# Work at the seam between two convs of a layer and in the closing sums: other engines, other order, other places

## The chip, the cores and the metric

The kernel runs on one core of a Trainium2 chip. The metric is the device time of one execution in microseconds. PE is TensorE, DVE is VectorE, ACT is ScalarE, POOL is GpSimd and SP is SyncE, which here issues nearly all DMAs.

## The reference

Two layers work on x of shape (4, 64, 256, 256). Each is `x = x + layer(gn(x))` with a group norm over pairs of channels. The change touches only layer 1:

```python
def _L1_conv_ref(x, ...):            # x is the normed input
    identity = x
    h = _conv3x3(x, _quantize_weight(w1), b1)
    h = relu(_batchnorm(h, gamma1, beta1))     # mean and variance over batch and space
    h = _conv3x3(h, _quantize_weight(w2), b2)
    h = _batchnorm(h, gamma2, beta2)
    return relu(h + identity)
x = x + _L1_conv_ref(_gn(x), ...)
```

Because a batch norm takes its mean over the whole batch, no value of the second conv can start before the first conv has ended, and no output before the second has.

## The kernel before

Rows of an image are handled in pairs; an image has 16 chunks of 8 row pairs, and a chunk is a tile of 128 partitions (two halves of 64 channels) by 8 x 256 numbers, 1 MiB. Chunks of the four images make 64 chunks. y is the result of layer 0, kept in HBM (`y_d`).

**First conv of layer 1.** It is laid out in `plan`, a table of steps and orders within a step (`at(step, order, call, ...)`), which five engines are then kept to. For each chunk: `conv1_differences` (GpSimd, L342), `conv1_upper_odd` and `conv1_upper` (ACT), `conv1_lower_odd` (DVE, L361) and `conv1_lower` (DVE, L352) build the tiles for PE; `conv1_odd` and `conv1_even` are the matmuls (L295), `conv1_shared` and `conv1_out` (L317, DVE) bring results to SBUF and add up the sums. `conv1_square` (ACT, Square at L381 with an accumulator) adds up the squares and issues the store of the chunk to `h1_d` from ACT's queue. After the last chunk of an image, `conv1_end` is one more row (six matmuls), `conv1_end_out` its result and its Square, and `conv1_close` reduces sums and squares (L388, L389). In before, the Square of the last chunk is placed behind the end row's.

**The seam.** `bn_affine(bn1, ...)` makes the scale and shift `ss1` of the first batch norm in a chain of small instructions on DVE, PE and ACT. Then the second conv starts. The first chunk has no earlier chunk to hide behind: its rows are scaled by `conv2_affine(0, "odd")` and `conv2_affine(0, "rest")` on ACT (L1264), GpSimd clears a pad row (L1267), `conv2_differences` makes two differences, one on DVE and one on GpSimd (L342), `conv2_upper_odd` copies the odd rows on ACT (L358), `conv2_lower_odd` (DVE, L361) makes the rounded remainder of the odd rows, `conv2_upper` and `conv2_lower` the same for the differences (L345, L350). PE's first three matmuls need the upper odd rows, the next nine the lower ones.

**Second conv.** A loop over 64 chunks in an order written out by hand for all five engines. The tiles for PE are six half tiles of 8256 bytes per partition (`diffs2`, `odds2`, for even and odd chunks) in a pool `halves2`, with `junk2` (the unread output of the Squares), `raw` and `m` tiles behind them. Results go to 14 places (`KEEP`); the first 50 chunks are also stored to `h2_d`, the last 14 stay in SBUF.

**The end.** After the second batch norm's scale `ss2` is known, every chunk becomes `y + relu(ss2 * h + shift + gn * y)`. The pool `end` takes the room of `halves2`, whose tiles it may overwrite one by one as they come free. y is loaded to three places of the ring of input tiles and to `MORE` places in `end`. The order over chunks starts with the 14 kept ones; for the others h is loaded from `h2_d`. SP issues in program order: a load that waits for its place holds up all behind it.

Of the kernel before, what the change touches and what calls it, by code (L numbers as in the profile page):

```python
# [41 lines left out]
def conv_preact_kernel(ctx: ExitStack, tc: tile.TileContext, io, col128, colset, col64):  # L42
# [25 lines left out]
    def flat(t):  # L68
        return t.rearrange("p a b -> p (a b)")
# [26 lines left out]
    def odd_tiles(pool, name, bufs, rows=CPAIR + 1):  # L96

        t = half_pads([half_tile(pool, f"odd_{name}", bufs, rows=rows)])[0]
        return [t[:, 4 * u : 4 * u + 4] for u in range(2)]

    def difference_tiles(pool, name, bufs, rows=CPAIR + 1):
        return half_pads([half_tile(pool, f"diff_{name}{u}", bufs, rows=rows) for u in range(2)])
# [17 lines left out]
    def at(step, order, call, *args):  # L120
        plan[step, order].append((call, args))
# [830 lines left out]
        if g:  # L952
            del m_in[b, k]

    def conv1_square(b, k):
        h = h_out.pop((b, k))
        square("h1", h[:, 1:, :] if k == 0 else h, junks[0], squares[b][:, k : k + 1])
        if k == 0:
            square("h1", h[0:C, 0:1, :], junks[0], squares[b][0:C, NCH : NCH + 1], slice(0, C))
        nc.scalar.dma_start(h1_d[b][:, k * CPAIR : (k + 1) * CPAIR, :], h)  # L960
# [220 lines left out]
    def plan_conv1(b):  # L1181
        t = CONV1 + b * (NG + 1)
        if b == 0:
            at(t - 4, -1, conv1_first)
            at(t, 12, conv1_open)
        for k in range(NCH):
            T = t + 4 * k
            places = [T + p for p in (-13, -7, -6, -5, -4, -4, -4, -3)]
            if b == 0 and k < 3:
                places = [t + p for p in ((-6, -3, -3, -2, -2, -2, -1, -1), (-4, -1, -1, 0, 0, 0, 0, 1), (-2, 1, 2, 3, 4, 4, 4, 5))[k]]  # L1190
            load, diff, odd, up0, up1, low_odd, low0, low1 = places

            first = b == k == 0

            def late(step, order):
                return (step, 5.5 + (order - 13) if step < t else order)

            at(load, 0, conv1_load, b, k)
            at(*late(diff, 13.08), conv1_differences, b, k)
            at(*late(odd, 13.36 if b == 0 and k == 3 else 13.1), conv1_upper_odd, b, k)  # L1200
            at(*late(up0, 13.12), conv1_upper, b, k, 0)
            at(*late(up1, 13.14), conv1_upper, b, k, 1)
            at(*late(low_odd, 13.2), conv1_lower_odd, b, k)
            at(*((t, 1.3) if first else late(low0, 13.22)), conv1_lower, b, k, 0)
            at(*((t, 1.32) if first else late(low1, 13.24)), conv1_lower, b, k, 1)
            at(T, 1.9 if first else 13, conv1_odd, b, k)
            at(T + 4 / 3, 13, conv1_even, b, k, 0)
            at(T + 4 / 3, 13.15, conv1_shared, b, k)
            at(T + 8 / 3, 13, conv1_even, b, k, 1)
            at(T + 8 / 3, 13.05, conv1_out, b, k, 0)  # L1210
            at(T + 4, 13.05 if k < NCH - 1 else 12.9, conv1_out, b, k, 1)
            at(T + 4 + 4 / 3, 13.16, conv1_square, b, k)
        at(t + NG, 12.95, conv1_end, b)
        at(t + NG + 1, 13.06, conv1_end_out, b)
        at(t + NG + 3, 13.3, conv1_close, b)
# [39 lines left out]
    def conv2_load(i):  # L1255
        b, k = chunks[i]
        h = h_in[i] = dense_in(f"h_{b}_{k}", CPAIR + 1)
        nc.sync.dma_start(h, h1_d[b][:, k * CPAIR : (k + 1) * CPAIR + 1, :])

    def conv2_affine(i, part=None):  # L1260
        b, k = chunks[i]
        (even, odd), _ = second_rows(h_in[i])
        for rows in {None: (h_in[i],), "odd": (odd,), "rest": (even, h_in[i][:, CPAIR, :])}[part]:
            nc.scalar.activation(rows, rows, AF.Relu, bias=ss1[:, 1:2], scale=ss1[:, 0:1])  # L1264
        if part != "odd":
            if k == 0:
                nc.gpsimd.memset(h_in[i][C:P, 0, :], 0.0)  # L1267
            if k == NCH - 1:
                nc.gpsimd.memset(h_in[i][0:C, CPAIR, :], 0.0)

    def conv2_differences(i, engines=(nc.gpsimd, nc.gpsimd)):
        for n, engine in enumerate(engines):
            raw_in[i, n] = halves_pool.tile([P, 4, W], F32, tag="raw", name=f"d2_{i}_{n}", bufs=2)
            differences(second_rows(h_in[i])[n], raw_in[i, n], engine)
# [7 lines left out]
    def conv2_upper_odd(i):  # L1282
        upper_odd(odds2[i % 2], second_rows(h_in[i])[1][0])
# [10 lines left out]
    kept = ctx.enter_context(tc.tile_pool(name="kept", bufs=1, reuse_waits="tile"))  # L1294
    halves_stack = ExitStack()
    halves_pool = halves_stack.enter_context(tc.tile_pool(name="halves2", bufs=1, reuse_waits="tile"))
    diffs2 = [difference_tiles(halves_pool, f"2{i}", 6, CPAIR) for i in range(2)]
    odds2 = [odd_tiles(halves_pool, f"2{i}", 6, CPAIR) for i in range(2)]
    junk2 = halves_pool.tile([P, CPAIR * W], BF16, name="junk_2")
    h2, h2_place = {}, count()  # L1300

    def chunk_h2(b, k):
        n = next(h2_place) % KEEP
# [6 lines left out]
    def conv2_odd(i):  # L1310
        b, k = chunks[i]
        if k == 0:
            totals_open(b)
        open_m[i] = bank("ap"[i % 2], f"ps_h2m_{i}")
        convolve_odd(open_m[i], "w2", odds2[i % 2])
# [29 lines left out]
    with tc.manual_schedule(  # L1345
        engines={
            mybir.EngineType.PE,
            mybir.EngineType.SP,
            mybir.EngineType.DVE,
            mybir.EngineType.Pool,  # L1350
            mybir.EngineType.Activation,
        }
    ):
        n = len(chunks)
        conv2_affine(0, "odd")
        conv2_upper_odd(0)
        conv2_affine(0, "rest")
        conv2_differences(0, (nc.vector, nc.gpsimd))
        conv2_lower_odd(0)
        conv2_upper(0, 0)  # L1360
        conv2_upper(0, 1)
        conv2_affine(1)
        conv2_lower(0, 0)
        conv2_lower(0, 1)
        conv2_differences(1)
        conv2_upper_odd(1)
        for i in range(n):
            conv2_odd(i)
            if i:
                conv2_out(i - 1, 1)  # L1370
            if i + 3 < n:
                conv2_load(i + 3)
            if i + 1 < n:
                conv2_upper(i + 1, 0)
                conv2_upper(i + 1, 1)
                conv2_lower_odd(i + 1)
                conv2_lower(i + 1, 0)
                conv2_lower(i + 1, 1)
            if i + 2 < n:
                conv2_affine(i + 2)  # L1380
                conv2_differences(i + 2)
            conv2_shared(i)
            if i:
                conv2_square(i - 1)
            conv2_even(i, 0)
            conv2_out(i, 0)
            if i + 2 < n:
                conv2_upper_odd(i + 2)
            conv2_even(i, 1)
        conv2_square(n - 1, 0, 4, 1)  # L1390
        conv2_out(n - 1, 1)
        conv2_square(n - 1, 4, CPAIR)

    steps = chunks[-KEEP:] + chunks[:-KEEP]
    shift = const.tile([P, B], F32, name="shift")
    ss2 = const.tile([P, 2], F32, name="ss2")
    y_of = {}

    halves_stack.close()
    end = ctx.enter_context(tc.tile_pool(name="end", bufs=2, reuse_waits="tile"))  # L1400
    MORE = 6
    AHEAD = 3 + MORE - 1

    def end_load(i):
        b, k = steps[i]
        if i % (3 + MORE) < 3:
            y_of[i] = dense_in(f"y_end_{b}_{k}", CPAIR)
        else:
            y_of[i] = end.tile([P, CPAIR, W], F32, tag="y", name=f"y_end_{b}_{k}", bufs=MORE)
        nc.sync.dma_start(y_of[i], y_d[b][:, k * CPAIR : (k + 1) * CPAIR, :])  # L1410

    for i in range(AHEAD):
        end_load(i)
    bn_affine(bn2, "g2", "be2", ss2, "bn2")
    for b in range(B):
        nc.vector.tensor_scalar(shift[:, b : b + 1], gn2[b][:, 2:3], ss2[:, 1:2], None, ALU.add)
    for i, (b, k) in enumerate(steps):
        if i + AHEAD < len(steps):
            end_load(i + AHEAD)
        y, h = y_of.pop(i), h2.pop((b, k))  # L1420
        v = end.tile([P, CPAIR, W], F32, tag="v", name=f"v_{b}_{k}")
        nc.scalar.activation(v, y, AF.Identity, bias=shift[:, b : b + 1], scale=gn2[b][:, 1:2])  # L1422
        nc.vector.scalar_tensor_tensor(h, h, ss2[:, 0:1], v, ALU.mult, ALU.add)  # L1423
        nc.vector.scalar_tensor_tensor(h, h, 0.0, y, ALU.max, ALU.add)
        nc.sync.dma_start(io["out"][b, k], flat(h))

        j = i - 3 + KEEP
        if i >= 3 and j < len(steps):
            b2, k2 = steps[j]
            nc.sync.dma_start(chunk_h2(b2, k2), h2_d[b2][:, k2 * CPAIR : (k2 + 1) * CPAIR, :])  # L1430

def _packed(parts, rows):

# [107 lines left out]
```

## Time and profile before

| | |
|---|---|
| time before, median of 3 runs | 3026.77 us (3007.64 to 3039.1) |
| profiled execution | 3016.92 us |
| its span | 3015.1 us |
| PE busy | 2357.4 us (78%) |
| DVE busy | 2478.0 us (82%) |
| ACT busy | 2054.8 us (68%) |
| POOL busy | 1676.3 us (56%) |
| DMA, mean over the span | 304 GB/s, 915.35 MB |

In the profile, times are microseconds from the start of the span. A line of the timeline gives start, duration, engine, source line, operation, output and inputs with shapes, the number of merged instructions and, in brackets, the idle time before it and what ended it. A line of a stretch gives its bounds and length, busy time and instruction count of PE, of weight loads, of DVE, ACT and POOL, then PE's granted clock, the mean busy share of the 16 DMA engines and GB/s. A line of the waits gives who waited for whom, the total, the number of times and the longest.

### The profile page before, as it was taken

To read this page: it belongs to the slowest core of one execution; us is meant where nothing else is said; L and a number is where in the kernel's file an instruction comes from. 1 tells how busy PE (TensorE), PEld (TensorE's weight loads), DVE (VectorE), ACT (ScalarE), POOL (GpSimd) and SP (SyncE) were. 2 spreads that over 40 slices of the span, in tenths; PEclk is the share of its full clock that TensorE was granted. 3 is DMA by queue.
4 is the path that set the end of the run, shared out by engine and by line. 5 is a ranking of instruction groups with operands and counts; after the bars stand their busy time and mean duration, and the time that the engine had idled before them with its cause. 6 is when DMAs were issued, how large, how long until landed. Compare 5 with 4: busy or idle time off the path is not lost.

```text
span 3015.1 us, 52987 instructions
## 1 busy us (share of the span) xinstructions
PE 2357.4 (78%) x21576; PEld 1503.4 (50%) x21576; DVE 2478.0 (82%) x2793; ACT 2054.8 (68%) x2274; POOL 1676.3 (56%) x1210
## 2 busy tenths in 40 slices
PE   1898899998999999988999999989999999000000
PEld 1444444444544445546666667867888888000000
DVE  5678688888888999968988989979999898876665
ACT  6898887787876555557667667868888887422222
POOL 5888887776877778744445546635555555000000
PEclk9999999999999999998999999989999999555555
DMA  8565479999999879848999897746777764899999
GB/s 345 191 249 224 184 259 376 350 342 352 336 343 324 303 288 326 293 147 310 366 356 352 321 345 300 267 178 255 263 266 264 265 232 144 351 411 409 421 427 409
DMA packets 135572, 915.35 MB, mean 304 GB/s; under 512 B 14944, under 2 KB 15712, under 8 KB 40608
## 3 DMA queue, kind: packets, MB, share of 16 engines
q1 hardware_dynamic: 126112, 844.85, 75.0%
q10 hardware_dynamic: 9216, 67.11, 5.5%
q8 instruction: 169, 2.77, 0.4%
q14 instruction: 75, 0.61, 0.1%
HBM read 573.74 MB, written 338.17 MB: 302 GB/s over the span
## 4 chain that ended last, share of the span: by engine, by line
PE 28%; DMA 18%; DVE 5%; issue 2%; ACT 1%; POOL 0%; SPq 0%; DVEq 0%; ACTq 0%; POOLq 0%
PE ps_h L295 18%; PE ps_h2m L295 6%; DMA y_end<-y_d 5%; DMA h<-h_d 4%; DMA out<-h 4%; PE ps_hm L295 3%; DMA y<-in_xp 2%; DVE diff L352 1%; PE ps_o L492 1%; DMA y_d<-y 1%; DVE h L317 1%; DMA h_d<-h 1%; DMA yn<-y_d 1%; DMA xs_in<-xs_d 1%; DVE odd L361 1%
## 5 line engine op out<-in xcount | busy, mean ns | idle before, releaser
L295 PE MATMUL ps_h<-diff,w_q 128*128 128x512 f32 x3072 | 753.8, 400 | 14.3 <-DVE h L317 13.7
L295 PEld LDWEIGHTS ps_h<-diff,w_q 128*128 128x128 f32 x3072 | 576.6, 189 | 192.1 <-issue 23.7
L492 PE MATMUL ps_c<-v,us 64*64 64x256 f32 x9216 | 544.6, 385 | 42.2 <-DVE ps_c L623 36.4
L342 POOL TENSOR_TENSOR d<-yn 128x1024 f32<-128x1024 f32 x128 | 356.0, 2801 | 305.3 <-DMA yn<-y_d 188.5
L492 PEld LDWEIGHTS ps_c<-v,us 64*64 64x64 f32 x9216 | 361.3, 136 | 200.4 <-DVE ps_c L623 45.6
L342 POOL TENSOR_TENSOR d<-h 128x1024 f32<-128x1024 f32 x127 | 311.9, 2477 | 194.8 <-DVE diff L350 133.4
L492 PE MATMUL ps_a<-h,av 64*64 64x512 f32 x4080 | 386.8, 492 | 34.8 <-DVE t L686 23.9
L317 DVE SCALAR_TENSOR_TENSOR h<-ps_h,scale_w,m 128x1024 f32<-128x1024 f32 x256 | 322.8, 1279 | 76.6 <-PE ps_h L295 53.9
L540 POOL TENSOR_TENSOR x<-x 128x512 f32<-128x512 f32 x256 | 329.9, 1289 | 12.3
L1422 ACT ACTIVATE v<-y_end,shift,gn 128x2048 f32<-128x2048 f32 x64 | 133.8, 2092 | 285.1 <-DMA y_end<-y_d 249.9
L492 PEld LDWEIGHTS ps_a<-h,av 64*64 64x64 f32 x4080 | 154.2, 133 | 302.6 <-issue 195.6
L381 ACT ACTIVATE junk<-h,less_h 128x2048 bf16<-128x2048 f32 (+3 forms) x133 | 256.0, 1925 | 11.1 <-DVE h L317 11.0
L1423 DVE SCALAR_TENSOR_TENSOR h<-h,ss,v 128x2048 f32<-128x2048 f32 x64 | 149.8, 2349 | 126.1 <-ACT v L1422 102.1
L683 DVE SCALAR_TENSOR_TENSOR t<-ps_a,m,t 128x1020 f32<-128x1020 f32 x128 | 163.3, 1276 | 103.1 <-ACT t L677 101.1
L848 DVE SCALAR_TENSOR_TENSOR y<-ps_o,ob,y 128x1024 f32<-128x1024 f32 x128 | 163.7, 1279 | 80.6 <-DMA y<-in_xp 27.4
L677 ACT ACTIVATE t<-ps_a,tap_bias,m 128x1024 f32<-128x1024 f32 x128 | 154.0, 1203 | 97.5 <-PE ps_a L492 96.9
L705 ACT ACTIVATE xs<-t 128x1024 f32<-128x1024 f32 x128 | 134.9, 1054 | 116.8 <-DVE t L689 86.8
L352 DVE SCALAR_TENSOR_TENSOR diff<-d,gn,diff 128x1024 fp32r<-128x1024 f32 x128 | 208.5, 1658 | 0.3 <-ACT diff L345 0.3
L295 PE MATMUL ps_hm<-odd,w_q 128*128 128x512 f32 x768 | 194.0, 402 | 8.6 <-ACT m L311 6.0
L295 PE MATMUL ps_h2m<-odd,w_q 128*128 128x512 f32 x768 | 193.2, 400 | 8.2 <-DVE odd L361 4.4
L345 ACT ACTIVATE diff<-d 128x1024 fp32r<-128x1024 f32 x128 | 135.1, 1055 | 83.4 <-POOL d L342 82.2
L532 POOL TENSOR_TENSOR x<-x,x 128x512 f32<-128x512 f32 x128 | 160.7, 1278 | 43.3 <-ACT x L526 43.3
(226 smaller groups left out, 4306.5 us busy)
## 6 DMA issues: line engine op xcount, KB each, us to landing
x<-in_xc SPq DMA_DIRECT2D x64, 1280.0 KB
h<-h_d SPq DMA_DIRECT2D x64, 1152.0 KB
yn<-y_d SPq DMA_DIRECT2D x60, 1152.0 KB
xs_in<-in_xp SPq DMA_DIRECT2D x64, 1024.0 KB
xs_d<-xs SPq DMA_DIRECT2D x128, 512.0 KB
xs_in<-xs_d SPq DMA_DIRECT2D x64, 1024.0 KB
y<-in_xp SPq DMA_DIRECT2D x64, 1024.0 KB
y_d<-y SPq DMA_DIRECT2D x64, 1024.0 KB
```

Source lines behind the costliest of these rows:

```text
L295: nc.tensor.matmul(ps, wq[w][:, kind, kx, :], t[:, rows, kx : kx + W], start=(j == 0), stop=(j == len(terms) - 1))
L317: nc.vector.scalar_tensor_tensor(h.rearrange("p (e k) w -> p e (k w)", e=2), ps.rearrange("p e k w -> p e (k w)"), w_scale[w], m.unsqueeze ...
L342: engine.tensor_tensor(raw.rearrange("p (g r) w -> p g r w", g=2), *pair, ALU.subtract)
L352: nc.vector.scalar_tensor_tensor(lower, raw, scale, upper.bitcast(F32), ALU.mult, ALU.subtract)
L381: nc.scalar.activation(junk[rows, 0:n], flat(h), AF.Square, bias=less[name][rows], accum_out=total)
L492: last[:] = [nc.tensor.matmul(ps[o, at_out[0] : at_out[1], :], w[i], rhs[i], **flags)]
L532: nc.gpsimd.tensor_tensor(x4[:, j - 1], x_rows(u, j + 2), x4[:, j - 1], ALU.subtract)
L540: nc.gpsimd.tensor_tensor(x[:, r : r + 2], x[:, r + 2 : r + 4], x[:, r : r + 2], ALU.subtract)
L677: nc.scalar.activation(flat(t), flat(ps), AF.Identity, bias=tap_bias, scale=sh[:, 1:2])
L683: nc.vector.scalar_tensor_tensor(t[:, :, 1:W], ps[:, :, 0 : W - 1], sh[:, 0:1], t[:, :, 1:W], ALU.mult, ALU.add)
L848: nc.vector.scalar_tensor_tensor(y, ps.rearrange("p x s w -> p x (s w)"), out_bias[b], y, ALU.add, ALU.add)
L1423: nc.vector.scalar_tensor_tensor(h, h, ss2[:, 0:1], v, ALU.mult, ALU.add)
```

## The change

At the first conv's end, the last chunk's Square is made in two halves, each placed right behind the result it reads and ahead of the end row; the second half issues the store. At the start of the second conv, the first chunk's even rows and last row are scaled and cut off at zero on DVE (`conv2_affine_vector`), which also clears the pad row and makes both differences; ACT keeps the odd rows. The half tiles are allocated in another order, odd tiles ahead of the difference tiles of the same parity.

At the end, the two-input sum with a scaled y (`v`) is replaced: with `inverse = ss2 / gn` the first sum is `h * inverse + y` in place of h, ACT then makes `relu(gn * that + shift)` in place, and the second sum adds y. The tile `v` is gone and y has 8 places in `end` in place of 6. Reciprocal and copy for the new scales are done at chunk 8 of the second conv. The first chunk of the end is done in halves, and the order of SP, DVE and ACT is now written out: the first sum of chunk i+1 goes ahead of the second sum of chunk i.

```diff
-    def conv1_square(b, k):
+    def conv1_square(b, k, part=None):
+        if part is not None:
+            h = h_out[b, k][:, 4 * part : 4 * part + 4, :]
+            square("h1", h, junks[0], squares[b][:, k + 2 * part : k + 2 * part + 1])
+            if part:
+                nc.scalar.dma_start(h1_d[b][:, k * CPAIR : (k + 1) * CPAIR, :], h_out.pop((b, k)))
+            return
...
-            at(T + 4 + 4 / 3, 13.16, conv1_square, b, k)
+            if (b, k) == (B - 1, NCH - 1):
+                at(T + 4, 12.85, conv1_square, b, k, 0)
+                at(T + 4, 12.92, conv1_square, b, k, 1)
+            else:
+                at(T + 4 + 4 / 3, 13.16, conv1_square, b, k)
...
+    def conv2_affine_vector(i):
+
+        (even, _), _ = second_rows(h_in[i])
+        for rows in (even, h_in[i][:, CPAIR, :]):
+            nc.vector.tensor_scalar(rows, rows, ss1[:, 0:1], ss1[:, 1:2], ALU.mult, ALU.add)
+            nc.vector.tensor_scalar(rows, rows, 0.0, None, ALU.max)
+        nc.vector.memset(h_in[i][C:P, 0, :], 0.0)
...
-    diffs2 = [difference_tiles(halves_pool, f"2{i}", 6, CPAIR) for i in range(2)]
-    odds2 = [odd_tiles(halves_pool, f"2{i}", 6, CPAIR) for i in range(2)]
+    diffs2, odds2 = [], []
+    for i in range(2):
+        odds2.append(odd_tiles(halves_pool, f"2{i}", 6, CPAIR))
+        diffs2.append(difference_tiles(halves_pool, f"2{i}", 6, CPAIR))
...
+    def end_scales():
+        for b in range(B):
+            nc.vector.reciprocal(inverse[:, b : b + 1], gn2[b][:, 1:2])
+            nc.vector.tensor_copy(shift[:, b : b + 1], gn2[b][:, 2:3])
...
         conv2_affine(0, "odd")
+        conv2_affine_vector(0)
+        conv2_differences(0, (nc.vector, nc.vector))
         conv2_upper_odd(0)
-        conv2_affine(0, "rest")
-        conv2_differences(0, (nc.vector, nc.gpsimd))
         conv2_lower_odd(0)
...
         for i in range(n):
+            if i == 8:
+                end_scales()
...
-    MORE = 6
+    MORE = 8
     AHEAD = 3 + MORE - 1
...
+    def end_sum(i):
+
+        b = steps[i][0]
+        h, y = h2[steps[i]], y_of[i]
+        for a, e in end_parts(i):
+            at_h = h[:, a:e, :]
+            nc.vector.scalar_tensor_tensor(at_h, at_h, inverse[:, b : b + 1], y[:, a:e, :], ALU.mult, ALU.add)
+            nc.scalar.activation(at_h, at_h, AF.Relu, bias=shift[:, b : b + 1], scale=gn2[b][:, 1:2])
+
+    def end_out(i):
+        b, k = steps[i]
+        h, y = h2.pop((b, k)), y_of.pop(i)
+        for a, e in end_parts(i):
+            at_h = h[:, a:e, :]
+            nc.vector.tensor_tensor(at_h, at_h, y[:, a:e, :], ALU.add)
+            nc.sync.dma_start(io["out"][b, k, :, a * W : e * W], flat(at_h))
...
-    for b in range(B):
-        nc.vector.tensor_scalar(shift[:, b : b + 1], gn2[b][:, 2:3], ss2[:, 1:2], None, ALU.add)
-    for i, (b, k) in enumerate(steps):
-        if i + AHEAD < len(steps):
+    nc.vector.tensor_scalar(inverse, inverse, ss2[:, 0:1], None, ALU.mult)
+    nc.vector.tensor_scalar(shift, shift, ss2[:, 1:2], None, ALU.add)
+    with tc.manual_schedule(
+        engines={mybir.EngineType.SP, mybir.EngineType.DVE, mybir.EngineType.Activation}
+    ):
+        end_sum(0)
+        for i in range(len(steps)):
+            if i + 1 < len(steps):
+                end_sum(i + 1)
             end_load(i + AHEAD)
-        y, h = y_of.pop(i), h2.pop((b, k))
-        v = end.tile([P, CPAIR, W], F32, tag="v", name=f"v_{b}_{k}")
-        nc.scalar.activation(v, y, AF.Identity, bias=shift[:, b : b + 1], scale=gn2[b][:, 1:2])
-        nc.vector.scalar_tensor_tensor(h, h, ss2[:, 0:1], v, ALU.mult, ALU.add)
-        nc.vector.scalar_tensor_tensor(h, h, 0.0, y, ALU.max, ALU.add)
-        nc.sync.dma_start(io["out"][b, k], flat(h))
-
-        j = i - 3 + KEEP
-        if i >= 3 and j < len(steps):
-            b2, k2 = steps[j]
-            nc.sync.dma_start(chunk_h2(b2, k2), h2_d[b2][:, k2 * CPAIR : (k2 + 1) * CPAIR, :])
+            end_out(i)
+            j = i - 3 + KEEP
+            if i >= 3 and j < len(steps):
+                b, k = steps[j]
+                nc.sync.dma_start(chunk_h2(b, k), h2_d[b][:, k * CPAIR : (k + 1) * CPAIR, :])
```

More of the change, by code (lines that the diff above doesn't have):

```diff
@@ L1296, in conv_preact_kernel @@
     halves_pool = halves_stack.enter_context(tc.tile_pool(name="halves2", bufs=1, reuse_waits="tile"))
-    diffs2 = [difference_tiles(halves_pool, f"2{i}", 6, CPAIR) for i in range(2)]
-    odds2 = [odd_tiles(halves_pool, f"2{i}", 6, CPAIR) for i in range(2)]
+    diffs2, odds2 = [], []
+    for i in range(2):
+        odds2.append(odd_tiles(halves_pool, f"2{i}", 6, CPAIR))
+        diffs2.append(difference_tiles(halves_pool, f"2{i}", 6, CPAIR))
     junk2 = halves_pool.tile([P, CPAIR * W], BF16, name="junk_2")
     h2, h2_place = {}, count()
+    inverse = const.tile([P, B], F32, name="inverse")
+    shift = const.tile([P, B], F32, name="shift")
+    def end_scales():
+        for b in range(B):
+            nc.vector.reciprocal(inverse[:, b : b + 1], gn2[b][:, 1:2])
+            nc.vector.tensor_copy(shift[:, b : b + 1], gn2[b][:, 2:3])
     def chunk_h2(b, k):
@@ L1394, in conv_preact_kernel @@
     steps = chunks[-KEEP:] + chunks[:-KEEP]
-    shift = const.tile([P, B], F32, name="shift")
     ss2 = const.tile([P, 2], F32, name="ss2")
@@ L1400, in conv_preact_kernel @@
     end = ctx.enter_context(tc.tile_pool(name="end", bufs=2, reuse_waits="tile"))
-    MORE = 6
+    MORE = 8
     AHEAD = 3 + MORE - 1
     def end_load(i):
+        if i >= len(steps):
+            return
         b, k = steps[i]
@@ L1410, in end_load, with end_parts @@
         nc.sync.dma_start(y_of[i], y_d[b][:, k * CPAIR : (k + 1) * CPAIR, :])
+    def end_parts(i):
+        return ((0, CPAIR // 2), (CPAIR // 2, CPAIR)) if i == 0 else ((0, CPAIR),)
+    def end_sum(i):
[12 more added lines that the diff above has]
+            nc.sync.dma_start(io["out"][b, k, :, a * W : e * W], flat(at_h))
     for i in range(AHEAD):
```

## The prediction

> **What bounds the kernel now.** I read the page's slices first, then the chain of waits, then the two places the change touches by their timelines, waits and stretches.
>
> ```profile
> PE   1898899998999999988999999989999999000000
> DMA  8565479999999879848999897746777764899999
> GB/s 345 191 249 224 184 259 376 350 342 352 336 343 324 303 288 326 293 147 310 366 356 352 321 345 300 267 178 255 263 266 264 265 232 144 351 411 409 421 427 409
> ```
>
> A slice is 75.4 us. Until slice 34 PE is full; in the last six PE does nothing and DMA moves 351 to 427 GB/s. So there are two regimes: in the second conv a microsecond counts if PE waits for it; in the end only if the DMA engines stand still. The chain of waits agrees: matmuls to 2563.5, then only DMAs to the end.
>
> Between the convs PE has no conv work from 2008.7. This is the timeline there (start, duration, engine, what ended the idle time before):
>
> ```profile
> 2008.02 1.28 DVE L317 SCALAR_TENSOR_TENSOR h<-ps_h,scale_w,m 128x1024 f32<-128x1024 f32 x1 [1.47 <-PE ps_h L295]
> 2010.49 2.00 ACT L381 ACTIVATE junk<-h,less_h 128x2048 bf16<-128x2048 f32 x1
> 2012.61 0.19 DVE L389 TENSOR_REDUCE sum_h<-squares 128x1 f32<-128x34 f32 x1 [2.17 <-ACT junk L381]
> 2016.87 1.24 ACT L1264 ACTIVATE h<-h,ss 128x1024 f32<-128x1024 f32 x1 [0.81 <-DVE ss L1250]
> 2020.84 1.23 DVE L342 TENSOR_TENSOR d<-h 128x1024 f32<-128x1024 f32 x1 [4.00 <-POOL h L1267]
> 2021.01 3.25 POOL L342 TENSOR_TENSOR d<-h 128x1024 f32<-128x1024 f32 x1 [0.21 <-ACT h L1264]
> 2021.98 3.37 DVE L361 TENSOR_TENSOR odd<-h,odd 128x1024 fp32r<-128x1024 f32 x1
> 2025.40 4.21 PE L295 MATMUL ps_h2m<-odd,w_q 128*128 128x512 f32 x9 [4.44 <-DVE odd L361]
> ```
>
> Two steps stand out: VectorE waits 2.17 us for the last Square before the sums can close, and the first odd difference (L361) takes 3.37 us beside GpSimd's difference. PE resumes at 2025.40, 8.5 us after the scale `ss` is there (2016.84).
>
> At the end the DMA share (the column before GB/s) falls once all loads are in:
>
> ```profile
> 2563.00:2566.00 3.00, 3.00 (x15) 2.39 (x14) 1.35 (x1) 1.22 (x2) 0.00 (x0) 1.00 0.34 145
> 2566.00:2569.00 3.00, 3.00 (x14) 2.18 (x12) 1.29 (x2) 1.24 (x2) 0.00 (x0) 1.00 0.00 0
> 2580.00:2582.00 2.00, 0.00 (x0) 0.00 (x0) 2.00 (x2) 1.56 (x2) 0.00 (x0) 0.50 1.01 426
> 2582.00:2584.00 2.00, 0.00 (x0) 0.00 (x0) 2.00 (x2) 1.83 (x2) 0.00 (x0) 0.50 0.22 90
> 2584.00:2586.00 2.00, 0.00 (x0) 0.00 (x0) 2.00 (x2) 1.76 (x1) 0.00 (x0) 0.50 0.00 0
> ```
>
> The first hole is loads that wait for a place, the second the wait for the first store. SP's own waits name the first:
>
> ```profile
> SPq L1410 <- DVE odd L361: 24.2, 3, 8.1
> SPq L1410 <- PE ps_h L295: 13.2, 3, 8.0
> ```
>
> Afterwards a step has three 1 MiB transfers and takes 7.37 us (stores issued at 2942.80 and 2950.16), 2.46 us each; in it VectorE works 4.64 us and ACT 2.09. Neither sets the pace.
>
> **The Trainium skill.** "DMA: Bandwidth & Descriptors", Where 436 GB/s comes from, gives a ceiling of 435 GB/s for the 16 engines; the trace's 427 from 2830 to 3010 is within 2% of it, so fewer instructions cannot shorten that stretch. "SBUF — State Buffer", Who interferes with whom: a VectorE operation with two SBUF inputs and a GpSimd one that reads SBUF exclude each other. The trace agrees: L361 takes 3.37 us here, 1.22 at least elsewhere. "TensorE: Matmul & The Clock Gate", What's actually happening: half clock after about 3.4 us of idling; here the nine matmuls take 0.47 us each, against 5.80/24 = 0.24 later. Price: "VectorE: DVE Perf Modes", The perf-mode tier table, has fp32 `tensor_scalar` from SBUF at twice the rate of `tensor_tensor`, 1227 ns for 2048 elements; the trace has only shorter ones or such as ran beside GpSimd.
>
> **The change, part by part.**
>
> *Squares in halves.* The first half's Square runs while PE does the last group. The second follows the last L317: 2009.30 + 0.09 + 1.15 (a half Square in the second conv's last chunk: 1.15) = 2010.54, then the end row's Square (0.50) and its accumulator read (0.18): the reduce starts near 2011.3 instead of 2012.61. ACT's issue of the store of h, between the two, can hold that up by 0.33. Gain 1.0 to 1.3; I take **1.2**. ACT was idle 4.22 us there, so the first half costs nothing.
>
> *First chunk on VectorE.* From `ss` on, before: ACT affine, odd tile, affine rest, GpSimd memset, differences, L361 ends after 8.5 us. Now on VectorE: multiply-add and max of 1024 elements, the same of 256, a memset, two differences, L361. By the skill's rate a 1024 `tensor_scalar` is (512+150)/0.96 = 0.69 us, a 256 one 0.29 (estimates from that page): 2 x 0.69 + 2 x 0.29 + 0.3 = 2.3. Then 2 x 1.23 + 1.22 = 3.7, together 6.0, say 6.2 with the waits between. At full-length rate (L313: 1.33 per 1024, from PSUM; 0.42 per 256, L910) the front part is 3.8 and the sum 7.5. ACT's own steps (1.24 and 1.06) are done by then. Gain 8.5 - 6.2 = **2.3**, low end 1.0. Moved behind it: the second Copy and the affine of chunk 1 on ACT, then GpSimd's differences of chunk 1. The affine began at 2025.26, 8.4 us after `ss`; now at about 6.0. So it advances with PE and no new wait comes up. Matmuls stay at half clock. From then on PE waited 0.8 us in the whole second conv, so the gain reaches its end.
>
> *Eight small VectorE instructions at chunk 8.* 8 x 0.2 = 1.6 us. VectorE is 99% busy there, but PE's next bank is ready early: even group at 2098.45, its bank read by 2096.53. 1.9 us of cover; I take 0, at worst 1.6.
>
> *Places at the end.* In the compiled program of before, a tag's first place is its lowest and the next go from its highest down. That puts the second y place over one of chunk 63's difference tiles, which is why the fifth load waited 8.0 us, to 2568.46. By the same rule the new order gives: first place over chunk 62's odd tile (free at 2555.1), second over raw tiles and chunk 62's m (2562), third over `junk_2`, which the last Square writes until 2571.7. SP issues in order, so loads 6 to 11 all wait for that Square. They then move without a gap, from 2572.5 for 6 x 2.46 = 14.8 us, to 2587.3. Before, nine loads were in at 2582.4, and by 2587.3 0.4 of a store: 9.4 transfers against 11. Gain 1.6 x 2.46 = **3.9 us**. The transfers number 64 + 50 + 64 as before. If the third place were not blocked, by 2590.8 it would be 14 against 11: gain 7.3; if the second were too, one transfer less: 1.4.
>
> *Other order of the sums.* Per chunk the same: one `scalar_tensor_tensor` (2.35), one ACTIVATE (2.09), and a `tensor_tensor` for the second sum (2.29). The scales take two instructions for four. First store: 2576.5 + 1.2 + 1.2 + 2.35 + 1.2 = 2582.5, against 2585.86, but the loads fill DMA until 2587.3, so the halves gain nothing. Now the store of chunk i stands behind the sum of i+1, which waits for its load: up to one step of 7.4 us. Stores already trail: chunk 55's is issued at 2974.72, some 30 us after its second sum. At the end 11 stores (27 us) follow the last load, which lands 20 us after issue; three VectorE operations (6.9) make the last one ready just then, with eight transfers in flight as cover. Cost 0.
>
> *Sum.* 1.2 + 2.3 + 3.9 = 7.4 us. The profiled execution took 3016.9 (span 3015.1): 3009.5. It lies 9.9 below the median shown, so on the median's scale 3026.8 - 7.4 = **3019**.
>
> **Rivals.**
>
> *A, loads earlier.* The third place is free before the last Square. For: it is a rule read from other tiles. Against: it explains the fifth load exactly. 1.2 + 2.3 + 7.3 = 10.8: 3016.
>
> *B, little at the seam.* VectorE's affine at full-length rate (1.0), the small instructions not covered (-1.6), ACT's DMA issue in the way (1.0), the end 3.9: -4.3: 3022. For: VectorE is nearly full in chunks 1 to 10. Against: the 1.9 us at PE's bank.
>
> *C, slower: the end's transfer rate.* It was 412 GB/s from 2660 to 2830 and 427 after, with the same three kinds of transfers; so it depends on something the trace doesn't name, perhaps which addresses lie in flight together, and loads of y two chunks further ahead change that. The end's 181 MB took 435 us busy, 416 GB/s. At 388 (the lowest stretch of ten us, 2630 to 2640) it is 467: +32 - 7.4: 3051. It decides below 409 GB/s, 1.7% under. Against: each kind has 1 MiB pieces as before.
>
> **How the numbers follow.** Forecast 0.55, A 0.20, B 0.13, C 0.12. The forecast's unknown costs span 3015 to 3024; runs of one kernel spread over 3007.6 to 3039.1, so 3000 to 3040 holds it, A, B and the mild part of C. 1% is 30 us, about what a measurement of this kernel can tell from no change. PE's whole idling at the seam and the holes at the end add up to less than that, so faster by over 1% needs luck of the runs: 0.03. Slower by over 1% is C's far end: 0.06. Within: 0.91.
>
> **What would show it.** The reduce of the squares about 2.0 us after the last L317 of the first conv ends, instead of 3.3; the first chunk's L361 near 1.22; PE resuming 6.2 us after `ss`; five y loads issued before the last Square and six right after it; DMA share at 1.0 from then on; 7.37 us a step. Wrong: a PE wait near chunk 8, a share below 1 in the steps after 2600, or a rate below 409.

## The result, and the profile after

| | before | after |
|---|---|---|
| median of 22 runs each, side by side | 3018.41 us (3007.64 to 3039.1) | 3007.57 us (3001.94 to 3022.28) |
| profiled execution | 3016.92 us, span 3015.1 | 3007.01 us, span 3005.2 |

The ratio is 0.9967, with a 95% interval of 0.9956 to 0.9978: about 10 us less. A second series with the same changed kernel, 22 runs against 59 of before, gave 0.9976 [0.9966, 0.9985], about 7 us. The forecast was 7.4 us less. Its absolute number, 3019 us, is 11 us too high, because it started from a median of three runs (3026.77) that lies 8 us above the median of 22.

I cut each profiled execution at two points that every version has: the end of the last L317 of the first conv, and the end of PE's last conv matmul.

| us | before | after |
|---|---|---|
| start to the last L317's end | 2009.30 | 2010.55 |
| from there to PE's end (seam and second conv) | 559.83 | 555.96 |
| from PE's end to the last store | 445.97 | 438.69 |

The first row, which the change hardly touches, lay anywhere from 2005 to 2019 us over all profiled versions; only the other two rows say something about the change: -3.9 and -7.3 us. The third contains the rate at which the DMAs happened to run, as experiment 1 shows.

The page's slices after:

```profile
DMA  8565479999998879858999987756777763899999
GB/s 347 191 246 224 185 260 374 351 340 351 321 345 325 313 267 328 298 184 292 354 365 346 340 321 299 277 208 238 261 274 261 266 238 140 356 409 425 426 426 410
```

Both regimes are as before. The seam, in the timeline of the changed kernel (start, duration, engine, what ended the idle time):

```profile
2009.27 1.28 DVE L317 SCALAR_TENSOR_TENSOR h<-ps_h,scale_w,m 128x1024 f32<-128x1024 f32 x1 [1.47 <-PE ps_h L295]
...
2010.65 1.15 ACT L381 ACTIVATE junk<-h,less_h 128x1024 bf16<-128x1024 f32 x1 [1.51 <-DVE h L317]
...
2012.55 0.19 DVE L389 TENSOR_REDUCE sum_h<-squares 128x1 f32<-128x34 f32 x1 [0.86 <-ACT junk L381]
...
2016.80 0.81 DVE L1274 TENSOR_SCALAR h<-h,ss 128x1024 f32<-128x1024 f32 x1
2017.65 0.69 DVE L1275 TENSOR_SCALAR h<-h 128x1024 f32<-128x1024 f32 x1
...
2018.26 0.41 DVE L1274 TENSOR_SCALAR h<-h,ss 128x256 f32<-128x256 f32 x1
2018.70 0.29 DVE L1275 TENSOR_SCALAR h<-h 128x256 f32<-128x256 f32 x1
...
2019.46 2.36 DVE L342 TENSOR_TENSOR d<-h 128x1024 f32<-128x1024 f32 x2
...
2021.74 1.22 DVE L361 TENSOR_TENSOR odd<-h,odd 128x1024 fp32r<-128x1024 f32 x1
2022.82 2.30 ACT L1282 ACTIVATE h<-h,ss 128x2304 f32<-128x2304 f32 x1
...
2023.01 4.02 PE L295 MATMUL ps_h2m<-odd,w_q 128*128 128x512 f32 x9 [2.12 <-DVE odd L361]
```

The last Square is a half one (1.15 us for 2.00), and the sums wait 0.86 us for it in place of 2.17. VectorE runs from `ss` (2016.77) to the odd difference without a wait; L361 takes 1.22 us with no GpSimd difference beside it; PE resumes at 2023.01, 6.24 us after `ss`, where it was 8.56. (The three matmuls that need only the upper odd rows run earlier, at 2019.24, and at 2019.31 in before.)

SP's waits around PE's end (2566.51):

```profile
SPq L1441 <- ACT junk L381: 9.3, 1, 9.3
...
SPq L1441 <- DVE h L317: 6.5, 1, 6.5
```

The second is the place over the raw tiles and m, which comes free with an L317 before PE's end. The first, 9.3 us, is the third place, over `junk_2`: SP stands until the last Square has ended, with five further loads behind it. And the stretches, by 2 us (the last columns are PE's granted clock, the DMA share, GB/s):

```profile
2558.51:2560.51 2.00, 2.00 (x11) 1.59 (x10) 0.87 (x2) 1.03 (x1) 0.00 (x0) 1.00 0.10 20
2560.51:2562.51 2.00, 2.00 (x10) 1.62 (x9) 1.34 (x1) 1.07 (x2) 0.00 (x0) 1.00 0.95 344
2562.51:2564.51 2.00, 2.00 (x11) 1.60 (x10) 0.79 (x1) 0.00 (x0) 0.00 (x0) 1.00 0.39 164
2564.51:2566.51 2.00, 2.00 (x9) 1.27 (x7) 0.50 (x2) 1.24 (x2) 0.00 (x0) 1.00 0.00 0
2566.51:2568.51 2.00, 0.00 (x0) 0.00 (x0) 1.48 (x3) 0.58 (x1) 0.00 (x0) 1.00 0.00 0
2568.51:2570.51 2.00, 0.56 (x2) 0.50 (x2) 0.63 (x4) 0.66 (x2) 0.00 (x0) 0.72 0.29 66
2570.51:2572.51 2.00, 0.59 (x2) 0.50 (x2) 1.10 (x8) 0.10 (x1) 0.00 (x0) 0.50 0.91 352
...
2578.51:2580.51 2.00, 0.00 (x0) 0.00 (x0) 2.00 (x2) 1.96 (x1) 0.00 (x0) 0.50 1.02 430
2580.51:2582.51 2.00, 0.00 (x0) 0.00 (x0) 2.00 (x2) 0.00 (x0) 0.00 (x0) 0.50 1.01 426
```

The first hole now runs from 2563 to 2570, and the second one, from 2582 to 2586 in before, is all but gone. The first store leaves SP 13.0 us after PE's end, 16.7 in before; loads of y are then still moving:

```profile
2579.50 1.47 SPq L1461 DMA_DIRECT2D out<-h  x2
```

### The profile page after: what moved, and what is told of

Its sections match the earlier page's. It is cut to its first block, busy times and chain, and to the rows that moved or that the text cites. A ratio compares the mean times of both kernels' runs of the same rounds, so it can differ in the third digit from the quotient of the medians.

```text
span 3005.2 us, 52876 instructions
## 1 busy us (share of the span) xinstructions
PE 2359.0 (78%) x21576; PEld 1505.5 (50%) x21576; DVE 2479.3 (82%) x2807; ACT 2054.4 (68%) x2275; POOL 1673.2 (56%) x1208
## 4 chain that ended last, share of the span: by engine, by line
PE 29%; DMA 18%; DVE 5%; ACT 1%; issue 1%; POOL 0%; SPq 0%; DVEq 0%; ACTq 0%; POOLq 0%
PE ps_h L295 19%; PE ps_h2m L295 6%; DMA y_end<-y_d 5%; DMA h<-h_d 4%; DMA out<-h 4%; PE ps_hm L295 3%; DMA y<-in_xp 2%; PE ps_o L492 1%; DMA y_d<-y 1%; DVE diff L352 1%; DVE h L317 1%; DMA h_d<-h 1%; DMA yn<-y_d 1%; DMA xs_in<-xs_d 1%; DVE h L1452 1%
## 5 line engine op out<-in xcount | busy, mean ns | idle before, releaser
L317 DVE SCALAR_TENSOR_TENSOR h<-ps_h,scale_w,m 128x1024 f32<-128x1024 f32 x256 | 322.8, 1279 | 74.2 <-PE ps_h L295 49.5
L540 POOL TENSOR_TENSOR x<-x 128x512 f32<-128x512 f32 x256 | 330.3, 1290 | 12.3
L1453 ACT ACTIVATE h<-h,shift,gn 128x2048 f32<-128x2048 f32 (+1 forms) x65 | 134.3, 2067 | 274.9 <-DVE h L1452 272.7
L1452 DVE SCALAR_TENSOR_TENSOR h<-h,inverse,y_end 128x2048 f32<-128x2048 f32 (+1 forms) x65 | 150.4, 2315 | 120.9 <-DMA y_end<-y_d 120.9
```

The source lines that it names most:

```text
L317: nc.vector.scalar_tensor_tensor(h.rearrange("p (e k) w -> p e (k w)", e=2), ps.rearrange("p e k w -> p e (k w)"), w_scale[w], m.unsqueeze ...
L540: nc.gpsimd.tensor_tensor(x[:, r : r + 2], x[:, r + 2 : r + 4], x[:, r : r + 2], ALU.subtract)
L1452: nc.vector.scalar_tensor_tensor(at_h, at_h, inverse[:, b : b + 1], y[:, a:e, :], ALU.mult, ALU.add)
```

## The experiments

For the end one number serves with each experiment: **idle DMA time around PE's end**, that is one minus the DMA share (a share above 1 counts as 1), added up over stretches of 1 us, in the 10 us before PE's end and in the 40 after it (the holes all lie in the first 20). Times to and from PE's end are from the profiled execution of each; ratios are against before, measured side by side, from 14 to 22 runs of the version; only the late store with eight places has no more than six.

**1. The seam alone** (squares in halves, first chunk on VectorE; the end as in before).

```diff
+                at(T + 4, 12.85, conv1_square, b, k, 0)
+                at(T + 4, 12.92, conv1_square, b, k, 1)
...
         conv2_affine(0, "odd")
+        conv2_affine_vector(0)
+        conv2_differences(0, (nc.vector, nc.vector))
         conv2_upper_odd(0)
-        conv2_affine(0, "rest")
-        conv2_differences(0, (nc.vector, nc.gpsimd))
```

> Only the two edits between the convs; the end as before. If the sum's two seam terms hold (1.2 + 2.3 us, in the changed kernel's profile 1.3 + 2.3), the reduce of the squares comes 2.0 us after the last L317 of the first conv, PE resumes 6.2 us after ss, and the time falls by 3.5 us, ratio 0.9988; from PE's last conv matmul to the end of the span it stays at 446 us. If the gain comes from the end alone: ratio 1.000, although the seam is shorter, because the rest of the second conv gives it back.

Ratio 0.9989 [0.9972, 1.0005]; 555.89 us from L317's end to PE's end, 442.86 after. The seam is the changed kernel's to 0.1 us. The end, whose code is the old one, was 3 us shorter than in before, with the same holes (12.1 us idle, 11.8 in before). Most of that is a difference in rate. Stretches of 32, 58, 170 and 170 us from PE's end, the third and the fourth here:

```profile
2651.34:2821.34 170.00, 0.00 (x0) 0.00 (x0) 106.29 (x47) 47.72 (x23) 0.00 (x0) 0.50 1.01 421
2821.34:2991.34 170.00, 0.00 (x0) 0.00 (x0) 107.93 (x47) 48.13 (x23) 0.00 (x0) 0.50 1.01 426
```

In the third stretch this execution has 421 GB/s where before had 412, with the same instructions.

**2. The end alone** (new order of tiles, eight places, new sums; the seam as in before). Against the changed kernel:

```diff
-            if (b, k) == (B - 1, NCH - 1):
-                at(T + 4, 12.85, conv1_square, b, k, 0)
-                at(T + 4, 12.92, conv1_square, b, k, 1)
-            else:
-                at(T + 4 + 4 / 3, 13.16, conv1_square, b, k)
+            at(T + 4 + 4 / 3, 13.16, conv1_square, b, k)
...
-        conv2_affine_vector(0)
-        conv2_differences(0, (nc.vector, nc.vector))
         conv2_upper_odd(0)
+        conv2_affine(0, "rest")
+        conv2_differences(0, (nc.vector, nc.gpsimd))
```

> The changed kernel with the seam as before. If the end's term is 3.9 us as forecast: ratio 0.9987, and 442 us from PE's last conv matmul to the end. If the changed kernel's profile is typical (7.3 us): ratio 0.9976 and 439 us. Seam as before: PE resumes 8.5 us after ss.

Ratio 0.9996 [0.9982, 1.0011]: nothing to be told from no change, though up to 5 us less is inside the interval. The profile shows the end of the changed kernel: 9.1 us idle, 440.34 us. The seam is the old one, 559.54.

**3. The changed kernel with six places.** All but the two further places; this also removes the load that waits for `junk_2`.

```diff
-    MORE = 8
+    MORE = 6
```

> The changed kernel with 6 y places in the end pool in place of 8, so that no place lies over the Squares' unread output and 9 loads go ahead of the first store. Theory (count of transfers): loads 5 and 6 go out at about 2558 and 2561 and three at 2566.5 on the changed kernel's clock, all nine are in by about 2575, then a hole of some 4.5 us until the first store at 2579.5; by 2584.8 it has moved 11 transfers, as many as the changed kernel, so the same time within 1 us: ratio to before 0.997. Rival: the two further places are worth two transfers, 4.9 us: ratio 0.998. And if the rate of the middle of the end follows the lead of the y loads, it is 412 GB/s here as in before; if not, 421 as in the changed kernel or anything else.

Ratio 0.9973 [0.9961, 0.9986], idle 8.8 us (2.3 before PE's end, 6.5 after it, since the nine loads are in 8.4 us after PE's end and the first store comes at 13.0), 437.50 us. No loss: what is lost behind PE's end is won ahead of it. My forecast had put the end's whole gain on the eleven loads that these two places allow.

**4. The changed kernel with places in the order in which they come free.** The rival "loads earlier": tiles allocated one by one, so that the y places come free in the order in which they are asked for, eight loads of eleven before PE's end.

```diff
-    diffs2, odds2 = [], []
-    for i in range(2):
-        odds2.append(odd_tiles(halves_pool, f"2{i}", 6, CPAIR))
-        diffs2.append(difference_tiles(halves_pool, f"2{i}", 6, CPAIR))
...
+    odd0 = half2("odd_20")
+    m_odd = m_tile(1)
+    diffs_odd = [half2(f"diff_21{u}") for u in range(2)]
+    odd1 = half2("odd_21")
+    m2 = [m_tile(0), m_odd]
+    diffs2 = [[half2(f"diff_20{u}") for u in range(2)], diffs_odd]
...
```

> The changed kernel with the tiles under the y places laid out in the order in which they come free, the unread output of the Squares outside them: low to high odd tile of even chunks, m of odd chunks, difference tiles and odd tile of odd chunks, m and difference tiles of even chunks, raw tiles, junk. Theory: the fifth to eighth load go out from 2558 to 2561, the last three at 2566.5 to 2568 (the changed kernel's clock), all eleven are in by about 2576 in place of 2584.8, then a hole of 3.5 us until the first store; by 2584.8 it has moved 13 transfers in place of 11: 4.9 us faster than the changed kernel, ratio to before 0.995. Rival: the early loads only move the hole, or run at a lower rate: no gain, 0.997.

Ratio 0.9960 [0.9947, 0.9973], median 3005.04 us. The stretches from 4 us before PE's end (2566.26) on:

```profile
2562.26:2564.26 2.00, 2.00 (x11) 1.58 (x10) 0.77 (x1) 0.00 (x0) 0.00 (x0) 1.00 1.00 426
2564.26:2566.26 2.00, 2.00 (x9) 1.28 (x7) 0.52 (x2) 1.24 (x2) 0.00 (x0) 1.00 1.02 430
2566.26:2568.26 2.00, 0.00 (x1) 0.00 (x0) 1.48 (x3) 0.57 (x1) 0.00 (x0) 1.00 1.02 430
2568.26:2570.26 2.00, 0.56 (x2) 0.50 (x2) 0.63 (x4) 0.67 (x2) 0.00 (x0) 0.72 1.00 414
...
2576.26:2578.26 2.00, 0.00 (x0) 0.00 (x0) 2.00 (x2) 0.98 (x2) 0.00 (x0) 0.50 0.20 82
2578.26:2580.26 2.00, 0.00 (x0) 0.00 (x0) 2.00 (x2) 1.96 (x1) 0.00 (x0) 0.50 0.10 41
2580.26:2582.26 2.00, 0.00 (x0) 0.00 (x0) 2.00 (x2) 0.00 (x0) 0.00 (x0) 0.50 1.01 403
```

The hole at PE's end is gone: 0.5 us idle before it, in place of 5.2. What stays is 4.0 us afterwards, because the loads are all in before the first store. The ratios alone don't part this version from the changed kernel (their intervals overlap); the idle time does, 4.5 us in place of 9.3 in one execution of each. The 431.24 us from PE's end agree, but have a fast second stretch in them (422 GB/s).

**5. The new order of tiles alone**, with the old sums, six places and the old seam.

```diff
-    diffs2 = [difference_tiles(halves_pool, f"2{i}", 6, CPAIR) for i in range(2)]
-    odds2 = [odd_tiles(halves_pool, f"2{i}", 6, CPAIR) for i in range(2)]
+    diffs2, odds2 = [], []
+    for i in range(2):
+        odds2.append(odd_tiles(halves_pool, f"2{i}", 6, CPAIR))
+        diffs2.append(difference_tiles(halves_pool, f"2{i}", 6, CPAIR))
```

> The kernel before with only the new order of the half tiles; sums, places and seam as before. Theory (count of transfers): six loads are out before PE ends in place of four, all nine are in about 5 us sooner, but the first store still comes 16.7 us after PE's last conv matmul, so the hole ahead of it only grows from about 3.5 to about 9 us: ratio 1.000, 443 to 446 us from PE's end to the end of the span. Rival: loads that go earlier are worth their transfers, two times 2.46: ratio 0.9984, 438 to 441 us.

Ratio 0.9995 [0.9982, 1.0008], 447.59 us. The loads do come earlier (2.1 us idle before PE's end for 6.9), but the first store still comes 16.5 us after it, so the hole ahead of it grows to 10.2: 12.3 in all. Earlier loads alone only move the hole.

**6. The new sums alone**, with six places, the old order of tiles and the old seam.

```diff
-        nc.scalar.activation(v, y, AF.Identity, bias=shift[:, b : b + 1], scale=gn2[b][:, 1:2])
-        nc.vector.scalar_tensor_tensor(h, h, ss2[:, 0:1], v, ALU.mult, ALU.add)
-        nc.vector.scalar_tensor_tensor(h, h, 0.0, y, ALU.max, ALU.add)
-        nc.sync.dma_start(io["out"][b, k], flat(h))
...
+            if i + 1 < len(steps):
+                end_sum(i + 1)
...
+            end_out(i)
```

> The kernel before with only the new sums (no v, first sum of the next chunk ahead, first chunk in halves, the new scales) but the old order of half tiles, 6 y places and the old seam. Theory: the nine loads are in 13.3 us after PE's end as before, the first half store now goes out 13.0 to 13.4 us after it in place of 16.7, so the hole closes: 3.3 us less, ratio 0.9989, 440 to 442 us from PE's end. Rival (the forecast's working: the earlier store is worth nothing, the two further places bring it): 443 to 446 us, ratio 1.000.

Ratio 0.9979 [0.9965, 0.9994], idle 6.9 + 1.6 = 8.5 us, 442.75 us. The loads are as late as in before, but the first store comes 13.0 us after PE's end (2578.95), just as they run out:

```profile
2574.95:2576.95 2.00, 2.00 (x11) 1.58 (x10) 0.78 (x1) 0.00 (x0) 0.00 (x0) 1.00 0.00 0
2576.95:2578.95 2.00, 2.00 (x9) 1.28 (x7) 0.51 (x2) 1.24 (x2) 0.00 (x0) 1.00 0.00 0
...
2588.95:2590.95 2.00, 0.00 (x0) 0.00 (x0) 2.00 (x2) 0.98 (x2) 0.00 (x0) 0.50 1.03 434
2590.95:2592.95 2.00, 0.00 (x0) 0.00 (x0) 2.00 (x2) 1.98 (x1) 0.00 (x0) 0.50 0.68 285
2592.95:2594.95 2.00, 0.00 (x0) 0.00 (x0) 2.00 (x2) 0.00 (x0) 0.00 (x0) 0.50 1.03 410
```

Of the second hole 0.6 us is left (share 0.68 over 2 us). So the earlier store can do alone what I had put on the places. Whether it is the halves or the new order of the sums that brings the store forward, no run separates.

**7. The best placement with the first store earlier still**: the sum of chunk 1 behind the first chunk's second sum.

```diff
-            if i + 1 < len(steps):
+            if 0 < i < len(steps) - 1:
                 end_sum(i + 1)
             end_load(i + AHEAD)
             end_out(i)
+            if i == 0:
+                end_sum(1)
```

> The kernel with the places laid out by when they come free, and the first chunk's second sum and stores ahead of the second chunk's first sum. Theory: the eleven loads are in 10.4 us after PE's end, the first half store goes out near 11.2 in place of 13.0 us, the hole shrinks from about 3.2 to 1.3 us: 2 us less than with the layout alone, some 430 us from PE's end, ratio to before 0.9955. Rival: ScalarE's half activations now stand in VectorE's way (VectorE waits for each of them) and the second store comes later by as much: no gain.

Ratio 0.9962 [0.9949, 0.9976], no better than experiment 4. The first store comes at 10.95 us, but the hole has only moved behind it, to 17 to 19 us after PE's end, and idle time is 4.2 us for 4.0. VectorE needs about 4.5 us for a chunk (first sum 2.34, second 2.28), and the second store came at 18.9, for 18.6 in experiment 4.

**8. The changed kernel again**, without an edit, beside before in a further series.

> The changed kernel itself once more, on the same chip as the three others. If the rate of the end's middle (170 us from 90 us after PE's end) belongs to the kernel, it is 421 to 422 GB/s again; if it belongs to the run, it may be 410 to 426. Ratio 0.9967.

Ratio 0.9976 [0.9966, 0.9985]; idle 9.1 us, 441.40 us from PE's end, for 438.69 the first time. The same code at 419 and 421 GB/s in the two long stretches, for 422 and 426.

**9 and 10. The first store late, with eight places and with six.** Experiments 3 and 6 left open what the places are for. In both kernels the first chunk is whole and the sums of chunks 1 and 2 go ahead of its second sum.

```diff
-        return ((0, CPAIR // 2), (CPAIR // 2, CPAIR)) if i == 0 else ((0, CPAIR),)
+        return ((0, CPAIR),)
...
-            if i + 1 < len(steps):
+            if i != 1 and i + 1 < len(steps):
                 end_sum(i + 1)
+            if i == 0:
+                end_sum(2)
```

The version with six places has this line besides:

```diff
-    MORE = 8
+    MORE = 6
```

With eight places:

> The changed kernel with its first store made late: chunk 0 whole instead of in halves, and the sums of chunks 1 and 2 placed before its second sum; everything else, the eight places of y included, stays. By the durations (three scalar_tensor_tensor of 2.35 and a second sum of 2.28 from the scales on) the first store is issued some 16.2 us after PE's end instead of 13.0. Theory (either cover closes the hole): with eight places the loads of y fill the DMA until some 18 us after PE's end, so the later store costs nothing: 9.1 us of DMA idle around PE's end (5 before it, 4.2 after) as in the changed kernel, 440 us from PE's end to the end, ratio 0.997 to 0.998. Rival (the store's time alone counts, the places nothing): 3 us more idle, 7 after PE's end, 443 us, ratio 0.998 to 0.999.

With six:

> The same late first store with six places of y instead of eight. Both theories expect the hole back here: the loads are in some 9 us after PE's end, the first store comes at 16.2, so 9.5 us idle after PE's end (6.5 with the early store and six places), some 12 in all as in the kernel before, 443 us from PE's end to the end, ratio 0.998 to 0.999. The theory that either cover is enough wants 3 us more idle here than in late8; the rival wants the same in both.

In both the first store comes 16.2 us after PE's end. With eight places: ratio 0.9964 [0.9952, 0.9977], idle 4.7 + 4.1 = 8.7 us, 436.22 us. With six: 0.9987 [0.9977, 0.9997], idle 2.2 + 9.5 = 11.7 us, 443.47 us. The stretches 8 to 18 us after PE's end, first with eight places:

```profile
2575.28:2577.28 2.00, 0.00 (x0) 0.00 (x0) 2.00 (x3) 0.52 (x1) 0.00 (x0) 0.50 1.03 434
2577.28:2579.28 2.00, 0.00 (x0) 0.00 (x0) 2.00 (x2) 1.84 (x2) 0.00 (x0) 0.50 0.99 418
2579.28:2581.28 2.00, 0.00 (x0) 0.00 (x0) 2.00 (x2) 1.83 (x2) 0.00 (x0) 0.50 1.02 434
2581.28:2583.28 2.00, 0.00 (x0) 0.00 (x0) 2.00 (x1) 2.00 (x1) 0.00 (x0) 0.50 1.00 422
2583.28:2585.28 2.00, 0.00 (x0) 0.00 (x0) 2.00 (x2) 0.09 (x1) 0.00 (x0) 0.50 1.02 430
```

and with six:

```profile
2573.33:2575.33 2.00, 0.00 (x0) 0.00 (x0) 2.00 (x3) 0.53 (x1) 0.00 (x0) 0.50 0.16 66
2575.33:2577.33 2.00, 0.00 (x0) 0.00 (x0) 2.00 (x2) 1.84 (x2) 0.00 (x0) 0.50 0.00 0
2577.33:2579.33 2.00, 0.00 (x0) 0.00 (x0) 2.00 (x2) 1.83 (x2) 0.00 (x0) 0.50 0.00 0
2579.33:2581.33 2.00, 0.00 (x0) 0.00 (x0) 2.00 (x1) 2.00 (x1) 0.00 (x0) 0.50 0.00 0
2581.33:2583.33 2.00, 0.00 (x0) 0.00 (x0) 2.00 (x2) 0.08 (x1) 0.00 (x0) 0.50 0.55 225
```

The two intervals just meet, at 0.9977; the holes show the difference, in one profiled execution each. With a late store the two places are worth 3 us of idle time; with an early one nothing. Either of the two closes the second hole.

**All together.** Time saved should be 3.7 us where the seam is changed, plus what the end gains. By idle time, that is 12.0 (the mean of the four with the old holes) less the idle time. There is a more direct count: the MiB that the DMAs moved from 40 us before PE's end to 25 us after it, by the GB/s of such stretches. The total, to the end of the span, is 179.1 to 179.3 MiB in all twelve executions, so what has been moved by then need not be moved later. The four with the old holes moved 12.54 on the mean, and a MiB more is worth 2.46 us, a third of one of the end's steps.

| version | idle before + after PE's end, us | MiB by 25 us after it | saved by idle time | saved by MiB | measured, (1 - ratio) x 3017 |
|---|---|---|---|---|---|
| before | 6.9 + 4.9 | 12.40 | | | |
| order of tiles alone | 2.1 + 10.2 | 12.55 | -0.3 | 0.0 | 1.5 |
| seam alone | 6.9 + 5.2 | 12.53 | 3.6 | 3.7 | 3.3 |
| six places, late store | 2.2 + 9.5 | 12.67 | 4.0 | 4.0 | 3.9 |
| end alone | 4.9 + 4.2 | 14.15 | 2.9 | 4.0 | 1.2 |
| sums alone | 6.9 + 1.6 | 14.06 | 3.5 | 3.7 | 6.3 |
| the change, twice | 5.2 + 4.1; 4.9 + 4.2 | 14.15; 14.12 | 6.4; 6.6 | 7.7; 7.6 | 10.0; 7.2 |
| six places | 2.3 + 6.5 | 14.07 | 6.9 | 7.5 | 8.1 |
| eight places, late store | 4.7 + 4.1 | 14.34 | 7.0 | 8.1 | 10.9 |
| ordered places | 0.5 + 4.0 | 16.01 | 11.2 | 12.2 | 12.1 |
| ordered places, store first | 0.5 + 4.2 | 15.96 | 11.0 | 12.1 | 11.5 |

An interval is some 3 to 5 us to either side. Every sum by MiB lies in its interval; by idle time the first series of the change falls out, whose 6.4 is just under its lower end of 6.6. Both counts show the same three levels: idle times of 12, 9 and 4.6 us, or some 12.5, 14.1 and 16.0 MiB. Counted up to 40 us, the middle level has 1.3 to 1.9 MiB more than the lowest and the highest 3.3.

Idle time gives the change less because the share can be near 1 while little moves, as here in before, just after its first store:

```profile
2587.13:2589.13 2.00, 0.00 (x0) 0.00 (x0) 2.00 (x2) 0.00 (x0) 0.00 (x0) 0.50 1.04 332
2589.13:2591.13 2.00, 0.00 (x0) 0.00 (x0) 2.00 (x2) 0.80 (x1) 0.00 (x0) 0.50 1.01 270
2591.13:2593.13 2.00, 0.00 (x0) 0.00 (x0) 2.00 (x2) 1.83 (x2) 0.00 (x0) 0.50 0.94 262
```

Why the rate is so low there, no run shows.

## Why the prediction was right, and where not

*Squares in halves: 1.2 forecast, 1.3 measured.* The reduce of the squares started 2.00 us after L317's end, 3.31 in before. ACT's DMA issue (2010.70) ran beside the Square and held nothing up.

*First chunk on VectorE: 2.3 forecast, 2.3 measured* (8.56 less 6.24). The working holds line by line: a 1024 `tensor_scalar` with immediates took the 0.69 us estimated from the Trainium skill ("VectorE: DVE Perf Modes", The perf-mode tier table), a 256 one 0.29, the differences 1.18 each, L361 1.22. Only the multiply-add with two scalars from SBUF cost more: 0.81 and 0.41. Matmuls stayed at 0.45 us each (4.02 for nine), and chunk 1's affine began 6.05 us after `ss`, as said. That the gain reaches PE's end is shown: of the twelve profiled executions the eight with these two steps took 555.4 to 556.0 us from L317's end to PE's end, the four without (before among them) 558.7 to 559.8. The means differ by 3.7.

*Eight small instructions at chunk 8: 0 forecast.* PE waited 1.1 us for VectorE in the second conv after the seam, 0.8 in before: at most 0.3.

*The loads at the end* ran as traced beforehand: a place free early, one after L317, and a 9.3 us wait for the unread output of the last Square, then six loads in one go and a full DMA. 3.9 us were forecast (1.6 transfers), and 1.6 MiB more by 25 us after PE's end are 3.9 us. Some luck is in that: at 18.2 us, where the forecast counted, the changed kernel had moved 11.8 MiB and the four with the old holes 10.5 on the mean, 1.3 transfers; the rest came in the next 7 us, in the stretch of before shown last, whose low rate the forecast didn't expect. The profile pair shows 7.3 us for the whole end, but part of that is the rate in the long middle stretch, 422 GB/s for 412, and the seam's experiment had 421 with the old end.

*"The halves gain nothing, since the loads fill the DMA."* True beside eight places: the late store cost nothing there. But I took it for a statement on the sums as such, and it was one on the pair. With six places the early store closes the hole alone, and the places add nothing. The step that failed is the attribution: the time was right, but the two places, on which I had put the 3.9 us, cost nothing when taken out (14.1 MiB with six as with eight). I had worked out when loads end and when the store comes, and not gone on to ask what the one would do without the other.

*Rival A (the third place free before the last Square)* was not what the change did, but its price stands: 7.3 us for the end by the forecast; with ordered places idle time fell by 7.5, the MiB give 8.5, and the version ran at 0.9960.

*Rival B (little at the seam)* falls by the 3.7 us. *Rival C (a lower rate at the end)* falls too. The stretches from 2598 on in the changed kernel, second to fourth:

```profile
2598.51:2656.51 58.00, 0.00 (x0) 0.00 (x0) 58.00 (x27) 27.21 (x13) 0.00 (x0) 0.50 1.01 404
2656.51:2826.51 170.00, 0.00 (x0) 0.00 (x0) 108.95 (x48) 50.24 (x24) 0.00 (x0) 0.50 1.01 422
2826.51:2996.51 170.00, 0.00 (x0) 0.00 (x0) 97.89 (x44) 43.96 (x21) 0.00 (x0) 0.50 1.01 426
```

Only the short one is under the 409 GB/s named as the point of decision, and before had 410 there; the long ones are not. DMA share is at 1.0 throughout and a step of three transfers takes 7.40 us.

So the forecast's 7.4 us is 3.7 + 3.9 = 7.6 by its own terms with their measured sizes, and the two series gave 10 and 7. Both intervals hold it (6.6 to 13.3 and 4.5 to 10.3); that the first gave 2 to 3 us more has no cause that I can show. The prediction took 30 us for about what a measurement of this kernel can tell from no change; with 22 runs side by side it is 3 to 4.

## What to carry to other kernels

Where a queue must not run dry between two kinds of transfer, work out both ends of the hole: when the last load lands and when the first store is ready. An earlier store or more loads to fill the time may each close it, and both together pay only once (here 1.5, 1.8 and 1.6 MiB); loads that merely go earlier shift the hole (0.0). When tiles of one stage are laid over tiles of another and loads go out in order, lay them so that each place is free when its turn comes, and count outputs that nobody reads among the tiles that block: here one such tile held six loads for 9.3 us, and laying out all places anew saved 4.7 us more of idle time, where the end's edits had saved 3. To judge such a change, count what has been moved by a fixed time, and not only how busy the DMA was.

## What the runs showed of the hardware that I had not expected

A VectorE `tensor_scalar` that multiplies and adds with two scalars from SBUF took 0.12 us longer than one that takes the maximum with an immediate, at 1024 and at 256 elements alike (0.81 and 0.69, 0.41 and 0.29). It looks like a fixed price, not a rate. Whether the scalars or the second operation cost it, no run separates.

The rate of a full DMA differed between executions by as much as a part of the change was worth. In the stretch from 90 to 260 us after PE's end it was 412 GB/s in before and 421 with the same code there, which is 3.7 us; for the changed kernel from 32 to 90 us it was 404, and with only the tiles placed otherwise 422 in experiment 4 and 397 in experiment 7, though these two have the same tiles. The series ran on different chips, so this may be the chip or the execution. Nor is it shown that the kernel has no part in it: in the stretch from 90 to 260 us the eight executions with the new sums and the new order of tiles had 419 to 426 GB/s, the four others 412, 414, 415 and 421. The measured times don't ask for such a part, since the sums by MiB do without it.

One microsecond in 440 is 1 GB/s; so the time of the end alone, from one profile, can't judge a part worth 3 us. What was moved by 25 us after PE's end can: 14.1 MiB in both executions of the changed kernel.
